# A transformer block on one core: rows and TensorE transposes in the first stage, loads a stage ahead and pinned uses at the end of attention

## The chip, the core and the metric

The kernel runs on one core of a Trainium2 chip. The core has engines that work side by side: TensorE (PE in the profile: matmuls and transposes, with its weight loads as PEld), VectorE (DVE), ScalarE (ACT), GpSimd (POOL), and SyncE (SP), whose queue issues most of the DMA transfers. [...] The metric is the device time of one execution in microseconds (us); the kernel before takes 1751.1 us, the median of three runs (1748.06 to 1751.12).

## The reference

One block on 2048 tokens of width 1024, in fp32: single-head attention of width 256 and a gated feed-forward network (FFN) of width 2752, each between two layer norms, with a residual.

```python
qkv = einsum('bsc,cf->bsf', x, Wqkv) + bqkv          # q, k, v of width 256
attn = softmax(einsum('bqd,bkd->bqk', q, k) / sqrt(d))
out  = einsum('bqk,bkd->bqd', attn, v) @ Wo + bo
# the block:
x = x + layernorm(attention(layernorm(x)))
x = x + layernorm((silu(xt @ W_gate.T) * (xt @ W_up.T)) @ W_down.T)   # xt = layernorm(x)
```

## The kernel before

**Precision.** A matmul operand is kept as two fp32r parts, a high part (an ACT cast, L109) and a low part (the difference, on DVE, L110); `split` makes both. A product is three matmuls: high x high, high x low, low x high (`mm3`, L142; `mmc`, L625).

**Order.** The program is traced in Python, and the framework then orders each engine's queue by simulating the traced program (`schedule_with_timeline_sim`, L1038): an instruction may be moved ahead of one traced earlier on its engine. `tc.keep_in_program_order(ins)` forbids this for one instruction: it stays behind the one traced just before it on its engine. Before the change only the last products of the second FFN product are kept so (L827). Buffers are given by hand: the same SBUF tiles (`f4`, `f2p`, `a1`, `a2`, `kx`, `wvo`, `qa`, `qb`, `xb`, `wr`, `xe`) serve one stage after another, and the eight PSUM banks are named at each use.

**Stage 1** (L240 to L254 and L337 to L354) normalizes x, transposes it to `xT` (channels on partitions, 512 tokens wide, double buffered by group), and computes K, Q (`qk`) and V (`v_block`) for four groups of 512 tokens (`g`). Group 0 comes by rows: `prep1` loads a tile of 128 tokens, normalizes its rows (`norm_rows`: bn_stats and aggregate on DVE, epsilon and the power on POOL, then L129), transposes it with eight PE transposes against the identity (L137) into two banks, and splits these. Groups 1 to 3 go another way, while PE works on the group before: `stats1` loads each of four tiles by rows for the statistics alone, and stores mean and reciprocal deviation to DRAM (`mr_d`, L198); `load_mr` reads the 512 pairs back, broadcast to all partitions (L202); `prep1t` then takes x already transposed by the host (`xt`), eight pieces of 128 channels x 512 tokens, subtracts the mean (L209, on POOL for odd pieces), multiplies (L210) and splits. The low parts of four Q and K weight blocks and of half the V weights are made by POOL.

**Attention** (L919 to L962) is a loop over 16 blocks `i` of 128 queries. Stage `i` transposes the probabilities of block `i` (`turn`, L292), computes scores and softmax of block `i + 1`, transposes the result of block `i - 1` (`turn_o`, L309), multiplies the probabilities by V (`attend`, L300, L301, and the sum of two halves at L304), and projects block `i - 1` (`proj`). For the first eight blocks (`EARLY`) the first residual and both norms follow at once (`residual`), and `xpose` transposes the normalized rows for the FFN and stores them to `xT_d`; the other eight leave their projection in `at_d`, and are finished beside the FFN's first pass.

**FFN** (L976 to L1001) runs in two passes over 1024 tokens each, with a Strassen-like scheme: `gate_up` makes seven block products for gate and for up from sums of x blocks (B11, B21, B22, T1 to T4), `run_down` the second product. Nearly all matmuls are at L628. The first pass's x blocks are made at the end of attention: `first_x` (stages 11 to 14) loads two pieces of `xT_d`, splits B11 and B21 into `xb`, forms sums (`sum_x`, L421) and stores them to `xs_d`; in stage 14 `first_t2` and `first_t13` reload sums and split them into `qa`, `qb`, `kx`; after the loop `first_t4` does so for T4 and B22 into `a1`, which holds V until attention is over. Four buffers (`spare`) serve these ten reloads in turn. Weights come through a feeder that loads and splits as buffers come free; two of its places lie in `wvo`, which `proj` uses to the end.

**Side work of the first pass.** Beside each of ten pairs of `gate_up`, `down_weights` loads two blocks of the down weights, forms four sums and stores them to `td`. In pairs 1 to 8 `late_tokens` finishes one of the eight late blocks: `residual` and, a step later, `xpose`. Loads and first uses stand in the same job.

Of the kernel before, what the change touches and what calls it, by code (L numbers as in the profile page):

```python
# [15 lines left out]
P = 128  # L16
# [17 lines left out]
@with_exitstack  # L34
def block_kernel(ctx, tc, x, xt, wqk, wv, bqk, bv, wo, bo, wgu, wlast, wd, out):

# [41 lines left out]
    dram = ctx.enter_context(tc.tile_pool(name="dram", bufs=1, space=bass.MemoryType.DRAM))  # L78
    mr_d = [tl(dram, [G, 2], F32, f"mr_d{g}") for g in range(NG)]
    q_d = [tl(dram, [P, 2, G], F32, f"q_d{g}") for g in range(NG)]  # L80
# [30 lines left out]

    def norm_stats(halves):

        s = small_tile()
        for i, h in enumerate(halves):
            nc.vector.bn_stats(s[:, 6 * i : 6 * i + 6], h)  # L116
        nc.vector.bn_aggr(s[:, 12:14], s[:, 0:12])
        nc.gpsimd.tensor_scalar(s[:, 14:15], s[:, 13:14], EPS, None, ALU.add)
        nc.gpsimd.tensor_tensor(s[:, 15:16], s[:, 14:15], mhalf, ALU.pow)
        return s[:, 12:13], s[:, 15:16], s  # L120
# [31 lines left out]
    vt = a1.rearrange("p a b c -> p (a b c)").rearrange("p (k h d) -> p k h d", h=2, d=D)  # L152
    xin, wraw, qst = f4[0:3], f4[3:5], f2[0:2]
    vst = [f2[4][:, 0:D], f2[4][:, D:]]
# [6 lines left out]
    def load_x(t):  # L161
        nc.sync.dma_start(xin[t % 3], x[t * P : (t + 1) * P, :])

# [3 lines left out]
    def load_wqk(i):  # L167
        r = wraw[raw_n[0] % 2].rearrange("p (c f) -> p c f", f=P)
        raw_n[0] += 1
        nc.scalar.dma_start(r, wqk[i])  # L170
        split(wqk_s[i][:, :, 0, :], wqk_s[i][:, :, 1, :], r, nc.gpsimd)

    def load_wv(i):
        r = wraw[raw_n[0] % 2].rearrange("p (c f) -> p c f", f=D)
        raw_n[0] += 1
        nc.scalar.dma_start(r, wv[:, 4 * i : 4 * i + 4, :])
        split(wv_s[:, 4 * i : 4 * i + 4, 0, :], wv_s[:, 4 * i : 4 * i + 4, 1, :], r, nc.gpsimd if i else nc.vector)

    def prep1(t, banks):
        norm_rows(xin[t % 3], t == 2)  # L180
        transpose_rows(xin[t % 3], xT[(t // TB) % 2], t % TB, banks)
        if t + 3 < TB:
            load_x(t + 3)

    xin_n = [0]
    xp = f2[2:4] + [f4[2][:, 0:512], f4[2][:, 512:1024]]
    xp_n = [0]

    def stats1(t):
        xt_ = xin[xin_n[0] % 2]
        xin_n[0] += 1
        nc.sync.dma_start(xt_, x[t * P : (t + 1) * P, :])
        m, r, s = norm_stats([xt_[:, 0:512], xt_[:, 512:1024]])
        nc.gpsimd.tensor_copy(s[:, 16:17], m)
        nc.gpsimd.tensor_copy(s[:, 17:18], r)
        nc.sync.dma_start(mr_d[t // TB][(t % TB) * P : (t % TB + 1) * P, :], s[:, 16:18])  # L198

    def load_mr(g):  # L200
        b = wraw[g % 2].rearrange("p (t s) -> p t s", s=2)
        nc.sync.dma_start(b, mr_d[g].partition_broadcast(P))  # L202
        return b

    def prep1t(g, c, mr):
        p = xp[xp_n[0] % 4]
        xp_n[0] += 1
        nc.sync.dma_start(p, xt[g, c])
        (nc.gpsimd if c % 2 else nc.vector).tensor_tensor(p, p, mr[:, :, 0], ALU.subtract)  # L209
        nc.vector.tensor_tensor(p, p, mr[:, :, 1], ALU.mult)  # L210
        d = xT[g % 2][:, c, :, :]
        split(d[:, 0, :], d[:, 1, :], p)

# [32 lines left out]
    load_wv(1)  # L246
    load_x(2)
    nc.scalar.dma_start(bv_s, bv.partition_broadcast(P))
    nc.scalar.dma_start(bqk_s, bqk)
# [37 lines left out]
    def turn(i, j):  # L287

        b = bank[4 + j % 2]
        for n in range(4):  # L290
            k = 4 * j + n
            nc.tensor.transpose(b[:, n * P : (n + 1) * P], p_s[:, k * P : (k + 1) * P], ident)  # L292
        d = pT[i % 2][:, 4 * j : 4 * j + 4, :, :]
        split(d[:, :, 0, :], d[:, :, 1, :], b.rearrange("p (n q) -> p n q", n=4))
# [11 lines left out]
    def turn_o(i):  # L306
        b = bank[7][:, 0:D]
        for d in range(2):
# [14 lines left out]
    def residual(t, a, xt):  # L323

        if t >= EARLY:
            nc.sync.dma_start(a, at_d[t])
            nc.sync.dma_start(xt, x[t * P : (t + 1) * P, :])
        m, r, s = norm_stats([a[:, 0:512], a[:, 512:1024]])
        nc.gpsimd.tensor_scalar(s[:, 16:17], m, r, -1.0, ALU.mult, ALU.mult)
# [7 lines left out]
    for g in range(NG):  # L337
        for i in range(4):
            qk(g, i, bank[4 + i % 2])
            if g + 1 == NG:  # L340
                continue
            if i == 0:
                for tb in range(TB):
                    stats1((g + 1) * TB + tb)
                mr = load_mr(g + 1)
            else:
                for c in range(2 * i - 2, 2 * i):
                    prep1t(g + 1, c, mr)
        if 0 < g < NG - 1:
            for tb in range(TB):  # L350
                v_block(g, tb, bank[6 + tb % 2])
        if g + 1 < NG:
            for c in range(6, 8):
                prep1t(g + 1, c, mr)  # L354
    x0_pool.release()
# [82 lines left out]

    def first_x(cb, r1, r2):
        load_xq(r1, 0, cb)  # L440
        load_xq(r2, 1, cb)
        split_xq(xb, cb, r1)
        sum_x(r1, r2)
        nc.sync.dma_start(xs_d[cb][0], r1)
        nc.sync.dma_start(xs_d[cb][1], r2)

    def first_t13(cb, r):
        nc.sync.dma_start(r, xs_d[cb][1])
        split_xq(kx, cb, r)

    def first_t2(n, r):
        for i in range(2):
            nc.sync.dma_start(r[:, (L, R)[i]], xs_d[2 * n + i][0][:, L])
        split(q2[n][:, :, 0, :], q2[n][:, :, 1, :], two(r))

    def first_t4(cb, r):
        nc.sync.dma_start(r[:, L], xs_d[cb][0][:, R])
        nc.sync.dma_start(r[:, R], xT_d[1][(4 + cb) * P : (5 + cb) * P, :])
        split_xq(a1, cb, r)

# [288 lines left out]

    bg_tiles = Ring(f4[0:4])  # L750

    def down_weights(p):

        r1, r2, r3 = (bg_tiles.get() for _ in range(3))
        nc.sync.dma_start(r1, wd[p * P : (p + 1) * P, :])
        nc.sync.dma_start(r2, wd[(p + NPAIR) * P : (p + NPAIR + 1) * P, :])
        add(r3[:, R], r2[:, R], r1[:, R], ALU.subtract)
        add(r3[:, L], r1[:, R], r1[:, L], ALU.subtract)
        add(r1[:, L], r3[:, R], r1[:, L])
        add(r2[:, L], r2[:, L], r1[:, L], ALU.subtract)  # L760
        for n, t in (("T1", r3[:, L]), ("T3", r3[:, R]), ("T2", r1[:, L]), ("T4", r2[:, L])):
            nc.sync.dma_start(td[p][n], t)
        for r in (r1, r2, r3):
            bg_tiles.free(r)

    def late_tokens(t, banks, part):
        if part == 0:
            late_tokens.tiles = bg_tiles.get(), bg_tiles.get()
            residual(t, *late_tokens.tiles)
        else:  # L770
            xpose(t, *late_tokens.tiles, banks)
            for r in late_tokens.tiles:
                bg_tiles.free(r)

# [144 lines left out]
    for i in range(NT):  # L919
# [10 lines left out]
        if more:  # L930
            scores(i + 1, 2)
            scores(i + 1, 3)
            softmax(i + 1)
        if 3 <= i < EARLY + 3:
            xpose(i - 3, *pair[(i - 3) % 3], bank[4:6])
        if i < EARLY:
            nc.sync.dma_start(pair[i % 3][1], x[i * P : (i + 1) * P, :])
        if i > 0:
            turn_o(i - 1)
        attend(i)  # L940
        if i > 0:
            proj(i - 1)
            if i - 1 < EARLY:
                residual(i - 1, *pair[(i - 1) % 3])
        if EARLY + 3 <= i < EARLY + 7:
            cb = i - EARLY - 3
            first_x(cb, *room[cb % 2])
# [26 lines left out]
    feed.pump()  # L974

    for s in range(2):  # L976
# [65 lines left out]
```

## Time and profile before

The profile is of one execution. Its parts used below: busy time of each engine, a row of 40 slices of the span, groups of instructions by line, and single instructions in order of time with what ended the idle time before them.

| | before |
|---|---|
| median of three runs | 1751.1 us |
| the profiled execution | 1749.74 us |
| its span, first to last instruction | 1748.0 us |
| mean granted TensorE clock | 0.986 |
| busy PE, PEld | 1698.3 us (97%), 1390.2 us (80%) |
| busy DVE, ACT, POOL | 1107.3, 694.5, 137.4 us |
| POOL busy in the first 120 us | 49 us |
| share of L628 in the chain that ended last | 69% |
| first attention transpose (L292) | 179.36 us |
| first FFN matmul (L628) | 441.7 us |
| last stall before L628 runs without a break | ends at 496.65 us |

The page's two rows on TensorE give the busy tenths of each of 40 equal slices (43.7 us each), and the granted clock in tenths:

```profile
PE   8789999998889999999999999999999999999997
PEclk9899999999999999999999999999999999999999
```

A matmul row's mean is the time from start to end of one matmul; neighbours overlap, so their spacing is shorter. The clock is what the throttle granted: at half of it matmuls follow each other at about half the rate.

### The profile page before, as it was taken

How to read it: one execution, taken by the hardware profiler on the slowest of the kernel's cores; microseconds unless marked ns; L12 is line 12 of the kernel's file. 1: busy time of each engine (PE TensorE's matmuls, PEld its weight loads, DVE VectorE, ACT ScalarE, POOL GpSimd, SP SyncE). 2: the span in 40 equal slices, each digit the busy share in tenths (PEclk: the TensorE clock that was granted, in tenths of full speed). 3: DMA queues.
4: the chain of work that ended last, by engine and by line, in shares of the span. 5: the costliest groups of instructions: out<-in, count | busy, mean ns of one | idle time of the engine just before them, and what ended most of it. 6: DMA issues, size and time to landing. Idle time of an engine off the chain costs nothing.

```text
span 1748.0 us, 21019 instructions
## 1 busy us (share of the span) xinstructions
PE 1698.3 (97%) x7692; PEld 1390.2 (80%) x7692; DVE 1107.3 (63%) x1636; ACT 694.5 (40%) x1032; POOL 137.4 (8%) x208
## 2 busy tenths in 40 slices
PE   8789999998889999999999999999999999999997
PEld 6578888887778888888888888788888888888886
DVE  6682577757667777777458546875655565355458
ACT  3131455535434444443245444333333333244343
POOL 5320001100011111111000001100000000000001
PEclk9899999999999999999999999999999999999999
DMA  7741023346365556665447656732333223386664
GB/s 224 176 134 49 13 76 99 123 156 224 115 231 179 187 187 234 205 218 189 160 137 255 212 178 198 246 100 97 105 128 112 96 91 115 121 280 197 193 188 160
DMA packets 136056, 278.89 MB, mean 160 GB/s; under 512 B 15376, under 2 KB 31888, under 8 KB 135952
## 3 DMA queue, kind: packets, MB, share of 16 engines
q1 hardware_dynamic: 133216, 270.60, 47.7%
q10 hardware_dynamic: 2736, 6.95, 1.1%
q8 instruction: 60, 0.98, 0.2%
q14 instruction: 44, 0.36, 0.1%
HBM read 193.60 MB, written 83.90 MB: 159 GB/s over the span
## 4 chain that ended last, share of the span: by engine, by line
PE 86%; DMA 7%; DVE 5%; issue 1%; ACT 1%; POOL 0%; DVEq 0%; POOLq 0%; SPq 0%; ACTq 0%
PE bank L628 69%; PE bank L144 3%; PE bank L145 3%; PE bank L146 3%; PE bank L300 3%; PE bank L301 1%; PE bank L231 1%; PE bank L292 1%; DMA mr_d<-small 1%; PE bank L384 1%; DVE small L116 1%; DVE a L110 1%; DMA f<-xT_d 1%; PE bank L232 1%; DMA f<-wd 1%
## 5 line engine op out<-in xcount | busy, mean ns | idle before, releaser
L628 PE MATMUL bank<-a 128*128 128x512 f32 x1176 | 273.7, 390 | 0.0
L628 PEld LDWEIGHTS bank<-a 128*128 128x128 f32 x1176 | 220.7, 188 | 46.9
L110 DVE TENSOR_TENSOR a<-f2p,a 128x1024 fp32r<-128x1024 f32 (+2 forms) x122 | 137.3, 1126 | 101.3 <-ACT a L109 89.3
L628 PE MATMUL bank<-xb,a 128*128 128x512 f32 x816 | 197.3, 395 | 0.0
L641 DVE TENSOR_TENSOR xi<-bank,xi 128x512 f32<-128x512 f32 (+1 forms) x168 | 113.3, 685 | 114.5 <-PE bank L628 52.5
L628 PEld LDWEIGHTS bank<-xb,a 128*128 128x128 f32 x816 | 152.9, 188 | 37.1
L109 ACT CAST a<-f2p 128x1024 fp32r<-128x1024 f32 (+2 forms) x122 | 112.9, 928 | 160.6 <-PE bank L628 108.5
L628 PE MATMUL bank<-kx,a 128*128 128x512 f32 x648 | 158.2, 395 | 0.0
L628 PE MATMUL bank<-a,a 128*128 128x512 f32 x648 | 155.6, 392 | 0.0
L628 PEld LDWEIGHTS bank<-kx,a 128*128 128x128 f32 x648 | 121.5, 187 | 29.4
L628 PE MATMUL bank<-wvo 128*128 128x512 f32 x600 | 142.4, 390 | 0.0
L628 PEld LDWEIGHTS bank<-a,a 128*128 128x128 f32 x648 | 121.1, 188 | 26.0
L628 PEld LDWEIGHTS bank<-wvo 128*128 128x128 f32 x600 | 112.6, 188 | 24.4
L110 DVE TENSOR_TENSOR a<-f,a 128x512 fp32r<-128x512 f32 (+3 forms) x103 | 86.8, 847 | 69.3 <-ACT a L109 65.8
L109 ACT CAST a<-f 128x512 fp32r<-128x512 f32 (+3 forms) x103 | 76.2, 742 | 135.6 <-PE bank L628 100.9
L628 PE MATMUL bank<-a,wvo 128*128 128x512 f32 x384 | 96.3, 400 | 4.6 <-DVE xi L641 4.6
L300 PE MATMUL bank<-a,a 128*128 128x512 f32 x256 | 97.3, 412 | 2.6 <-ACT a L109 2.6
L110 DVE TENSOR_TENSOR wvo<-f2p,wvo 128x1024 fp32r<-128x1024 f32 (+2 forms) x47 | 53.4, 1137 | 63.2 <-ACT wvo L109 54.6
L110 DVE TENSOR_TENSOR a<-wr,a 128x1024 fp32r<-128x1024 f32 (+2 forms) x62 | 65.2, 1053 | 43.1 <-ACT a L109 26.1
L628 PE MATMUL bank<-kx,wvo 128*128 128x512 f32 x384 | 91.6, 390 | 0.0
L628 PEld LDWEIGHTS bank<-a,wvo 128*128 128x128 f32 x384 | 73.1, 191 | 22.4 <-DVE xi L641 5.0
L641 DVE TENSOR_TENSOR xi<-xi,xi 128x512 f32<-128x512 f32 x124 | 85.2, 687 | 3.6
(236 smaller groups left out, 2796.3 us busy)
## 6 DMA issues: line engine op xcount, KB each, us to landing
f2p<-wgu SPq DMA_DIRECT2D x43, 512.0 KB, 4.3
hd_S<-xi SPq DMA_DIRECT2D x80, 256.0 KB, 5.2
f<-x SPq DMA_DIRECT2D x30, 512.0 KB, 5.7
hd_A<-xi SPq DMA_DIRECT2D x60, 256.0 KB, 2.0
f<-wgu SPq DMA_DIRECT2D x21, 512.0 KB, 5.2
wr<-wgu SPq DMA_DIRECT2D x20, 512.0 KB, 5.3
f<-wd SPq DMA_DIRECT2D x20, 512.0 KB, 4.8
td_T<-f SPq DMA_DIRECT2D x40, 256.0 KB, 3.1
```

The lines of the kernel that those rows point to most:

```text
L109: nc.scalar.copy(hi, src)
L110: (lo_engine or nc.vector).tensor_tensor(lo, src, f32(hi), ALU.subtract)
L116: nc.vector.bn_stats(s[:, 6 * i : 6 * i + 6], h)
L144: nc.tensor.matmul(o, w[0], m[0], start=first, stop=False)
L145: nc.tensor.matmul(o, w[0], m[1], start=False, stop=False)
L146: nc.tensor.matmul(o, w[1], m[0], start=False, stop=last)
L231: nc.tensor.matmul(b, xg[:, c, 0, cols], wv_s[:, c, :, :].rearrange("p a f -> p (a f)"), start=(c == 0), stop=False)
L232: nc.tensor.matmul(b[:, D:], xg[:, c, 1, cols], wv_s[:, c, 0, :], start=False, stop=(c == 7))
L292: nc.tensor.transpose(b[:, n * P : (n + 1) * P], p_s[:, k * P : (k + 1) * P], ident)
L300: nc.tensor.matmul(b, p[:, k, 0, :], vt[:, k, :, :].rearrange("p h d -> p (h d)"), start=(k == 0), stop=False)
L628: one = nc.tensor.matmul(o, w[i], m[j], start=first and n == 0, stop=last and n == 2, skip_group_check=chained)
L641: nc.vector.tensor_tensor(o, a, b, op)
```

## The change

Stage 1 takes every group by rows. `stats1`, `load_mr`, `prep1t`, `mr_d` and the host's `xt` go; `prep1` serves all 16 tiles, four buffers of x are loaded at the start, and tile `t + 4` is loaded as soon as tile `t` has been transposed. The tiles of group `g + 1` are prepared one after each `qk(g, i)`. The epsilon is added on DVE, and all low parts of weights are made on DVE.

In attention the banks are dealt out anew: `turn` uses 4 and 7, `turn_o` 5, and `xpose`, now for block `i - 2` and after the projection, 6 and 5. The reloads for the first pass become objects with a `load` and a `use`; the uses are pinned. `first_x` is cut into `first_load`, a stage ahead, and `first_sums`. Four reloads are issued in stage 14 and used in stage 15 ahead of `attend(15)`; two are loaded and used right behind the loop, the last four behind `proj(15)`.

Beside the first pass, `load_down(p + 1)` and `residual` run in the second job of pair p (`behind`), while `xpose` of the block before, the loads for the next late block and the sums of `down_weights` run in its first job (`ahead`); `down_weights` works in place in two buffers, with its first subtraction pinned, and `residual` of late blocks has its bn_stats pinned.

```diff
-    def norm_stats(halves):
+    def norm_stats(halves, pin=None):
...
-            nc.vector.bn_stats(s[:, 6 * i : 6 * i + 6], h)
+            b = nc.vector.bn_stats(s[:, 6 * i : 6 * i + 6], h)
+            if pin:
+                pin(b)
...
-        nc.gpsimd.tensor_scalar(s[:, 14:15], s[:, 13:14], EPS, None, ALU.add)
+        nc.vector.tensor_scalar(s[:, 14:15], s[:, 13:14], EPS, None, ALU.add)
...
-    xin, wraw, qst = f4[0:3], f4[3:5], f2[0:2]
+    xin, wraw, qst = f4[0:4], [f4[4], f2p[1]], f2[0:2]
...
-        split(wqk_s[i][:, :, 0, :], wqk_s[i][:, :, 1, :], r, nc.gpsimd)
+        split(wqk_s[i][:, :, 0, :], wqk_s[i][:, :, 1, :], r)
...
     def prep1(t, banks):
-        norm_rows(xin[t % 3], t == 2)
-        transpose_rows(xin[t % 3], xT[(t // TB) % 2], t % TB, banks)
-        if t + 3 < TB:
-            load_x(t + 3)
...
+        r = xin[t % TB]
+        norm_rows(r, False)
+        transpose_rows(r, xT[(t // TB) % 2], t % TB, banks)
+        if t + TB < NT:
+            load_x(t + TB)
...
             qk(g, i, bank[4 + i % 2])
...
+            if g + 1 < NG:
+                prep1((g + 1) * TB + i, (bank[2 * (i % 2)], bank[2 * (i % 2) + 1]))
...
-        b = bank[4 + j % 2]
+        b = bank[(4, 7)[j % 2]]
...
-        b = bank[7][:, 0:D]
+        b = bank[5][:, 0:D]
...
+    def split_later(dst, src):
+        pin(nc.scalar.copy(dst[:, :, 0, :], src))
+        pin(nc.vector.tensor_tensor(dst[:, :, 1, :], src, f32(dst[:, :, 0, :]), ALU.subtract))
...
+    class First:
+        def __init__(self, dst, halves):
+            self.dst, self.halves = dst, halves
+        def load(self, r):
+            self.r = r
+            for h, d in zip((L, R), self.halves):
+                nc.sync.dma_start(r[:, h], d)
+        def use(self):
+            split_later(self.dst, two(self.r))
...
     def down_weights(p):
-        r1, r2, r3 = (bg_tiles.get() for _ in range(3))
-        nc.sync.dma_start(r1, wd[p * P : (p + 1) * P, :])
-        nc.sync.dma_start(r2, wd[(p + NPAIR) * P : (p + NPAIR + 1) * P, :])
-        add(r3[:, R], r2[:, R], r1[:, R], ALU.subtract)
...
+        r1, r2 = f4[0:2]
+        pin(nc.vector.tensor_tensor(r2[:, R], r2[:, R], r1[:, R], ALU.subtract))
...
-        if 3 <= i < EARLY + 3:
-            xpose(i - 3, *pair[(i - 3) % 3], bank[4:6])
...
             turn_o(i - 1)
+        if i == NT - 1:
+            for f in order[:4]:
+                f.use()
         attend(i)
         if i > 0:
             proj(i - 1)
...
+        if 2 <= i < EARLY + 2:
+            xpose(i - 2, *pair[(i - 2) % 3], (bank[6], bank[5]))
+        if 0 < i <= EARLY:
+            residual(i - 1, *pair[(i - 1) % 3])
+        cb = i - EARLY - 3
+        if 0 <= cb < 4:
+            first_sums(cb, *room[cb % 2])
+        if 0 <= cb + 1 < 4:
+            first_load(cb + 1, *room[(cb + 1) % 2])
...
+            order = [t2[0], t13[0], t13[1], t13[2], t2[1], t13[3]] + t4
             spare = f4[2], f4[3], wr[1], xe
-            for n in range(2):
-                first_t2(n, spare[n])
-            for cb in range(4):
-                first_t13(cb, spare[(2 + cb) % 4])
-    for cb in range(4):
-        first_t4(cb, spare[(2 + cb) % 4])
+            for f, r in zip(order, spare):
+                f.load(r)
+    for n in range(4, 6):
+        order[n].load(spare[n % 4])
+        order[n].use()
     turn_o(NT - 1)
     proj(NT - 1)
+    for n in range(6, 10):
+        order[n].load(spare[n % 4])
+        order[n].use()
...
+    def ahead(p):
+        if late(p - 1):
+            xpose(late(p - 1), *f4[2:4], Y[0:2])
+        if late(p):
+            nc.sync.dma_start(f4[2], at_d[late(p)])
+            nc.sync.dma_start(f4[3], x[late(p) * P : (late(p) + 1) * P, :])
+        down_weights(p)
+    def behind(p):
+        if p + 1 < NPAIR:
+            load_down(p + 1)
+        if late(p):
+            residual(late(p), *f4[2:4])
+    load_down(0)
...
-            jobs = []
-            if s == 0:
-                jobs.append(lambda: down_weights(p))
-                if 1 <= p < 1 + NT - EARLY:
-                    t = EARLY + p - 1
-                    jobs += [lambda: late_tokens(t, Y[0:2], 0), lambda: late_tokens(t, Y[0:2], 1)]
+            jobs = [] if s else [lambda: ahead(p), lambda: behind(p)]
```

More of the change, by code (lines that the diff above doesn't have):

```diff
@@ L34, in block_kernel @@
 @with_exitstack
-def block_kernel(ctx, tc, x, xt, wqk, wv, bqk, bv, wo, bo, wgu, wlast, wd, out):
+def block_kernel(ctx, tc, x, wqk, wv, bqk, bv, wo, bo, wgu, wlast, wd, out):
     nc = tc.nc
@@ L78, in block_kernel @@
     dram = ctx.enter_context(tc.tile_pool(name="dram", bufs=1, space=bass.MemoryType.DRAM))
-    mr_d = [tl(dram, [G, 2], F32, f"mr_d{g}") for g in range(NG)]
     q_d = [tl(dram, [P, 2, G], F32, f"q_d{g}") for g in range(NG)]
@@ L161, in load_x @@
     def load_x(t):
-        nc.sync.dma_start(xin[t % 3], x[t * P : (t + 1) * P, :])
+        nc.sync.dma_start(xin[t % TB], x[t * P : (t + 1) * P, :])
     raw_n = [0]
@@ L176, in load_wv @@
         nc.scalar.dma_start(r, wv[:, 4 * i : 4 * i + 4, :])
-        split(wv_s[:, 4 * i : 4 * i + 4, 0, :], wv_s[:, 4 * i : 4 * i + 4, 1, :], r, nc.gpsimd if i else nc.vector)
+        split(wv_s[:, 4 * i : 4 * i + 4, 0, :], wv_s[:, 4 * i : 4 * i + 4, 1, :], r)
     def prep1(t, banks):
-        norm_rows(xin[t % 3], t == 2)
-        transpose_rows(xin[t % 3], xT[(t // TB) % 2], t % TB, banks)
-        if t + 3 < TB:
-            load_x(t + 3)
[L187 to L212, printed above, removed]
+        r = xin[t % TB]
[3 more added lines that the diff above has]
+            load_x(t + TB)
     def qk(g, i, b):
@@ L247, in block_kernel @@
     load_x(2)
+    load_x(3)
     nc.scalar.dma_start(bv_s, bv.partition_broadcast(P))
@@ L323, in residual @@
     def residual(t, a, xt):
[L325 to L328, printed above, removed]
+        m, r, s = norm_stats([a[:, 0:512], a[:, 512:1024]], tc.keep_in_program_order if t >= EARLY else None)
         nc.gpsimd.tensor_scalar(s[:, 16:17], m, r, -1.0, ALU.mult, ALU.mult)
@@ L339, in block_kernel @@
             qk(g, i, bank[4 + i % 2])
[L340 to L348, printed above, removed]
+            if g + 1 < NG:
+                prep1((g + 1) * TB + i, (bank[2 * (i % 2)], bank[2 * (i % 2) + 1]))
         if 0 < g < NG - 1:
@@ L351, in block_kernel @@
                 v_block(g, tb, bank[6 + tb % 2])
-        if g + 1 < NG:
-            for c in range(6, 8):
-                prep1t(g + 1, c, mr)
     x0_pool.release()
@@ L436, in build_x, with first_load, first_sums @@
         split_x("T4", cb, r1[:, R])
-    def first_x(cb, r1, r2):
+    pin = tc.keep_in_program_order
+    def split_later(dst, src):
+        pin(nc.scalar.copy(dst[:, :, 0, :], src))
+        pin(nc.vector.tensor_tensor(dst[:, :, 1, :], src, f32(dst[:, :, 0, :]), ALU.subtract))
+    def first_load(cb, r1, r2):
         load_xq(r1, 0, cb)
         load_xq(r2, 1, cb)
-        split_xq(xb, cb, r1)
+    def first_sums(cb, r1, r2):
+        split_later(by_half(xb)[:, :, cb], two(r1))
         sum_x(r1, r2)
@@ L445, in first_x @@
         nc.sync.dma_start(xs_d[cb][1], r2)
[L447 to L459, printed above, removed]
+    class First:
[7 more added lines that the diff above has]
+            split_later(self.dst, two(self.r))
+    t13 = [First(by_half(kx)[:, :, cb], (xs_d[cb][1][:, L], xs_d[cb][1][:, R])) for cb in range(4)]
+    t2 = [First(q2[n], (xs_d[2 * n][0][:, L], xs_d[2 * n + 1][0][:, L])) for n in range(2)]
+    t4 = [First(by_half(a1)[:, :, cb], (xs_d[cb][0][:, R], xT_d[1][(4 + cb) * P : (5 + cb) * P, :])) for cb in range(4)]
     class Ring:
@@ L748, in gate_up_rest, with load_down @@
         nc.sync.dma_start(hl_d[s][1], g22[:FR, :])
-    bg_tiles = Ring(f4[0:4])
+    def load_down(p):
+        for r, fb in zip(f4[0:2], (p, p + NPAIR)):
+            nc.sync.dma_start(r, wd[fb * P : (fb + 1) * P, :])
     def down_weights(p):
-        r1, r2, r3 = (bg_tiles.get() for _ in range(3))
-        nc.sync.dma_start(r1, wd[p * P : (p + 1) * P, :])
-        nc.sync.dma_start(r2, wd[(p + NPAIR) * P : (p + NPAIR + 1) * P, :])
-        add(r3[:, R], r2[:, R], r1[:, R], ALU.subtract)
-        add(r3[:, L], r1[:, R], r1[:, L], ALU.subtract)
-        add(r1[:, L], r3[:, R], r1[:, L])
+        r1, r2 = f4[0:2]
+        pin(nc.vector.tensor_tensor(r2[:, R], r2[:, R], r1[:, R], ALU.subtract))
+        add(r1[:, R], r1[:, R], r1[:, L], ALU.subtract)
+        add(r1[:, L], r2[:, R], r1[:, L])
         add(r2[:, L], r2[:, L], r1[:, L], ALU.subtract)
-        for n, t in (("T1", r3[:, L]), ("T3", r3[:, R]), ("T2", r1[:, L]), ("T4", r2[:, L])):
+        for n, t in (("T1", r1[:, R]), ("T3", r2[:, R]), ("T2", r1[:, L]), ("T4", r2[:, L])):
             nc.sync.dma_start(td[p][n], t)
[L763 to L773, printed above, removed]
     def wd_half(fb, j):
@@ L942, in block_kernel @@
             proj(i - 1)
[L943 to L947, printed above, removed]
+        if 2 <= i < EARLY + 2:
[7 more added lines that the diff above has]
+            first_load(cb + 1, *room[(cb + 1) % 2])
         if i == NT - 4:
@@ L974, in block_kernel, with late @@
     feed.pump()
+    def late(p):
+        return EARLY + p if 0 <= p < NT - EARLY else None
+    def ahead(p):
[11 more added lines that the diff above has]
+    load_down(0)
     for s in range(2):
@@ L1022 @@
         "x": x.reshape(T, C),
-        "xt": x.reshape(NG, G, NC_, P).transpose(0, 2, 3, 1),
         "wqk": blocks(np.concatenate([w[:, D : 2 * D], w[:, :D]], axis=1)),
```

## The prediction

> **What bounds the kernel now.** I read the page's 40 slices first, for where TensorE (PE) is not full; then a table of windows over those stretches; then the waits of PE; then single rows of the timeline for what stands in front of a late instruction. In the slices PE reads 9 nearly everywhere, so only work that PE itself does, or time in which it does none, can change the end.
>
> The windows: length in us, then busy us (instructions) of PE, weight load, VectorE (DVE), ScalarE (ACT), GpSimd (POOL), then the granted clock, DMA share, GB/s.
>
> ```profile
> 40.00:60.00 20.00, 15.01 (x56) 11.05 (x54) 10.34 (x19) 1.68 (x3) 6.99 (x18) 0.91 0.79 156
> 60.00:80.00 20.00, 14.34 (x51) 10.52 (x52) 18.48 (x30) 5.98 (x10) 10.80 (x19) 0.82 0.63 161
> 80.00:100.00 20.00, 15.08 (x50) 11.72 (x50) 14.73 (x24) 4.41 (x9) 6.38 (x7) 0.76 0.60 157
> 180.00:380.00 200.00, 199.59 (x1105) 169.02 (x1103) 132.11 (x257) 101.33 (x208) 16.96 (x48) 1.00 0.27 85
> 380.00:400.00 20.00, 18.03 (x86) 14.82 (x85) 16.00 (x30) 7.08 (x16) 0.00 (x0) 0.91 0.73 263
> ...
> 420.00:440.00 20.00, 15.05 (x71) 12.12 (x71) 12.15 (x20) 9.74 (x19) 0.00 (x0) 0.83 0.48 158
> ...
> 460.00:480.00 20.00, 14.98 (x61) 11.25 (x60) 14.83 (x21) 10.24 (x15) 0.00 (x0) 0.91 0.66 218
> 480.00:500.00 20.00, 15.42 (x62) 12.20 (x61) 13.49 (x21) 7.06 (x10) 1.68 (x3) 0.91 0.57 192
> ```
>
> A window's loss is its idle PE time plus (1 - clock) x length: in the half-clock stretches the L300/L301 pairs follow each other at 0.64 us, elsewhere at 0.35. From 40 to 100 us: 6.8 + 9.3 + 9.7 = 25.8. From 380 to 500 us: 3.8 + 0 + 8.4 + 0 + 6.8 + 6.4 = 25.4. Counting matmuls at their warm spacing (0.233 us for 512 columns) gives 26 and 23. Attention proper, 180 to 380, loses 0.4, and 520 to 1700 nothing: the change can gain only in two places, and everything it adds to PE elsewhere is paid in full.
>
> What PE waited for (total us, times, longest):
>
> ```profile
> PE bank L144 <- DVE kx L221: 5.5, 3, 3.4
> PE bank L628 <- DVE xi L641: 4.6, 1, 4.6
> PE bank L309 <- DVE f L304: 4.4, 2, 2.7
> PE bank L144 <- ACT kx L220: 3.6, 1, 3.6
> ...
> PE bank L231 <- ACT a L109: 3.0, 1, 3.0
> PE bank L300 <- ACT a L109: 2.6, 1, 2.6
> ```
>
> The L144 and L231 waits lie in 40 to 100 us, the others in 380 to 500. None of the engines named is saturated there; each stood behind a transfer. In group order: the four `mr_d` stores and the broadcast reload land in 6.6 and 5.1 us after each x load's 5.7, so each group's statistics cost 17 us of DMA in series before `prep1t` may start.
>
> **Stage 1, removed.** Per group of 512 tokens DVE did 8 bn_stats and 4 aggregates (5.9 us), some 4 subtractions at L209 (1.13 us mean), 8 multiplications at L210 (0.78), 8 low parts (0.62): 21.7 us. The L209 and L210 means are stretched by POOL's share of L209, as the first row shows:
>
> ```profile
> 57.30 1.83 DVE L209 TENSOR_TENSOR f2p<-f2p,f 128x512 f32<-128x512 f32 x1 [2.73 <-DMA f<-mr_d]
> ...
> 24.84 1.09 PE L137 MATMUL bank<-ident,f 128*128 128x128 f32 x8
> 25.68 0.37 PE L232 MATMUL bank<-wvo,xT 128*128 128x256 f32 x1
> ```
>
> **Stage 1, put in.** Per 128 tokens: bn_stats 1.28, aggregate 0.20, an epsilon add now on DVE (some 0.1, the nearest row being L281's 0.15), L129 0.81, two low parts 1.3: 3.7 us, 14.7 a group. The pow stays on POOL, and ACT makes the same eight casts a group. x is loaded a whole group ahead (PE needs 22 to 37 us a group, a load 5.7), so the DMA chain is gone, and SP issues 39 transfers less (12 `mr_d`, 3 reloads, 24 `xt`). `load_x(t+4)` holds SP until tile t is transposed; behind it stand only q_d stores and later x loads. The first 2 us still ask for 2 MB of x (four loads for three and two `xt`). The five low parts of weights that POOL did come to DVE: 5 x 1.21 = 6 us, all before 40 us.
>
> PE gets 12 x 8 = 96 transposes. The rows above price them: eight occupy PE from 24.84 to 25.68, where the next matmul starts, 0.105 us each, so 10.1 us. [...] This trace also has a mean of 272 to 292 ns in its transpose rows, but as latency, overlapped by the neighbours. [...] And attention has 281 transposes (L292 195, L384 64, L309 22) between 180 and 380 with the clock at 1.00: mixed with matmuls they do not lower it. I take 10.1.
>
> What is late next: the border from group 0 to group 1. DVE starts at 6.3 us and owes 4 x 3.7 for group 0, 7.3 for weights, 5.0 for four V epilogues, 14.7 for group 1, 2.7 for Q and K epilogues: 44.5, so 50.8 without a pause, some 54 with 3 us of waiting for data. PE, at 48.3 when it ran dry before, has 3.4 us of transposes more: 51.7. I take 3 us of loss, with half-clock time 4 (ends 0 and 8). From there a group costs PE 37.0 us (24 x 4 x 0.233 + 11.2 + 3.4) and DVE 21 (14.7 + 5.0 + 1.3), so PE has the cover; 1 us (0 to 4). The first 20 us, 9.5 lost until the first x is normalized, stay.
>
> Stage 1: 25.8 - 4 - 1 - 10.1 = **10.7 us gained**. Ends: 25.8 - 0 - 10.1 = +16, and 25.8 - 12 - 10.1 = +4[...].
>
> **End of attention.** The waits one by one, by what stood ahead in the engine's queue:
> - 387.5, 1.97 us: DVE's L304 stood behind L421 waiting for `load_xq` (landed at 387.55). Loads go a stage (16.8 us of PE) ahead, against 4 to 6 us of landing: gone, with 1.8 us of half clock.
> - 423.3, 1.76 us: L304 stood behind low parts for T1, T3 and T2, 1.22 us each. Four of the six move to stage 15, behind `turn_o(14)`, two behind the loop: gone here.
> - 429.2, 2.6 + 0.6 us, and 3.4 of clock: ACT's pT cast stood behind a cast whose reload had not landed:
>
> ```profile
> 430.19 1.04 ACT L109 CAST kx<-f 128x1024 fp32r<-128x1024 f32 x1 [2.94 <-DMA f<-xs_d]
> 431.14 0.58 ACT L109 CAST a<-bank 128x512 fp32r<-128x512 f32 x1
> ```
>
>   Issued in stage 14, used in stage 15: gone.
> - 462.6, 2.7 + 0.5 us, and 1.8 of clock: L304 stood behind four T4 splits. They are pinned behind `proj(15)`: gone.
> - 470.5, 1.9 us: `g11`'s copy (L660) behind two casts of weights into `wvo`. Untouched; stays.
> - 492.1, 4.6 us, and 1.8 of clock: DVE in `gate_up`'s first pair stood behind `down_weights` and `residual`, whose loads were issued at their use (2.4 + 5.0 + 2.3 us of DVE waiting). With loads a half-pair or more ahead (PE needs 39 us a pair): gone.
>
> New waits: `order[4]` and `[5]` are loaded into `spare[0:2]` and used at once. ACT's cast waits for the landing, with `turn_o(15)`'s cast possibly behind it, and then `proj(15)`, the `wvo` slots and their weights. The load can start once use 0 is through DVE (1.05 + 1.22 us) and takes 4.3 us (longest 5.8), 8 in all; PE's cover is attend(15) and proj(14), 16 x 0.35 + 2.8 = 8.4, plus up to 48 products on B11 and B21 (11 us). Cost with cover 0; without it 5.8 and a 3.4 us half-clock window, 7.5. Six of the ten splits also crowd ACT and DVE just before FFN weights do. T4 is needed 28 us into the FFN, so 6 to 9 are covered. I take 4 (nearer the covered case, as the cover is ample), which with L660's 1.9 leaves about 6. The gain, from the smaller count: 23 - 6 = **17 us**; ends 7 and 22. On SP's queue `load_down(0)` must wait for the `at_d` stores from f4[0:2], but is used only a quarter pair later.
>
> The rest: `down_weights` keeps its four additions, `xpose` its transposes, `turn` and `turn_o` swap banks: 0, hidden by DVE's and ACT's idle third and half of attention.
>
> **Sum.** 10.7 + 17 = 27.7. The profiled execution took 1749.7 us (span 1748.0 and 1.7 around it): 1722. The median of the runs is 1.4 above it: **1723**.
>
> **Rivals.**
> - *Only stage 1 gains*: the pinned uses hold ACT and DVE in order before late data, and the end's stalls move behind the loop. For: two uses directly follow their loads. Against: the covers above. 10.7 + 3: **1737**.
> - *Only the end gains*: DVE becomes stage 1's bound (44.5 of 45 us at its start)[...]. Against: 14.7 us a group, less than the 21.7 of before. 17 + 0: **1734**.
> - *Slower: banks.* `turn` now shares bank 7 with `proj`, and `xpose` shares 6 with `attend` and 5 with `turn_o` and `proj`. If an evacuation (ACT 0.59 + DVE 0.68 = 1.3 us) is exposed at two of these handovers in 14 stages, 36 us come in where only 0.4 was lost: **1759**. It decides from 2.0 us a stage. Against: bank 5 had turns, proj and xpose before, with PE full at 16.8 us a stage.
> - *Everything goes*, nothing new waits: 16 + 22: **1713**.
>
> **How the numbers follow.** Forecast 0.58, with its own range 1714 to 1732; only stage 1 0.14; only the end 0.13; everything 0.05; banks 0.07; the gains just cancelled 0.03. Dropping the banks' 0.07, the cancelled 0.03 and the outer halves of others leaves 1712 to 1739. Two runs of this kernel can be told apart from some 0.2% (3.5 us) on: faster 0.90; the cancelled case splits into within 0.02 and slower 0.01, so slower is 0.08.
>
> **What would show it.** Right: 40 to 100 us with PE near 20 of 20 and clock 1.00, no `mr_d`, POOL nearly idle there, the first L292 some 10 us earlier; 0.1 us per L137; the start of solid L628 some 27 us earlier; none of the six waits but L660's. Wrong: DVE solid and PE waiting for xT's low parts up to 60 us; PE idle beside `turn_o` after the loop; any loss inside attention.

## The result, and the profile after

The changed kernel takes 1727.2 us (median of four runs, 1727.15 to 1728.61), the kernel before 1749.6 beside it. The ratio is 0.9875, 95% interval 0.9858 to 0.9892: 22 us or 1.25% faster. The forecast was 1723.

First the windows of the profile after (span 1726.8 us; columns as in the prediction):

```profile
20.00:40.00 20.00, 19.01 (x100) 15.41 (x100) 19.87 (x41) 8.91 (x15) 3.48 (x5) 1.00 0.55 185
40.00:60.00 20.00, 20.00 (x111) 16.97 (x110) 14.35 (x28) 6.24 (x12) 2.44 (x4) 1.00 0.21 69
60.00:80.00 20.00, 20.00 (x97) 16.41 (x96) 11.02 (x23) 2.90 (x6) 1.80 (x3) 1.00 0.19 64
...
180.00:360.00 180.00, 176.78 (x971) 148.25 (x971) 117.33 (x246) 88.81 (x185) 13.01 (x32) 1.00 0.29 94
...
440.00:460.00 20.00, 13.69 (x40) 9.65 (x40) 17.12 (x22) 12.41 (x17) 0.00 (x0) 0.66 0.67 231
460.00:480.00 20.00, 20.00 (x89) 16.29 (x88) 17.08 (x28) 9.33 (x14) 2.30 (x3) 1.00 0.65 232
```

Stage 1 is clean: PE is busy 20.00 us of every 20, at a granted clock of 1.00, from 40 to 160 us, and POOL is nearly idle. Of the losses before the FFN one hole is left, at 440 to 460: by the rule of the prediction 6.3 us idle and (1 - 0.66) x 20 = 6.8 us lost to the clock, 13.1 in all. And attention, which lost 0.4 us in 200, now idles 3.2 in 180.

The waits of PE in the same trace name both (total us, times, longest), and PE's rows in the hole show four pauses:

```profile
PE bank L604 <- ACT xi L636: 3.4, 1, 3.4
PE bank L138 <- DVE f L130: 3.3, 2, 3.0
PE bank L145 <- DVE oTs L109: 2.2, 2, 1.8
PE bank L275 <- ACT f L348: 2.0, 2, 1.4
```

```profile
442.44 0.44 PE L284 MATMUL bank<-ident,f 128*128 128x128 f32 x2 [0.26 <-DVE f L279]
443.82 0.50 PE L145 MATMUL bank<-wvo,oTs 128*128 128x512 f32 x1 [0.94 <-ACT oTs L108]
...
446.31 0.80 PE L145 MATMUL bank<-wvo,oTs 128*128 128x512 f32 x1 [1.76 <-DVE oTs L109]
...
454.29 2.93 PE L604 MATMUL bank<-qa,a 128*128 128x512 f32 x6 [3.35 <-ACT xi L636]
```

L604 is the FFN's matmul line now (L628 before), L636 is `g11`'s copy (L660), L145 to L147 are `mm3`, L284 is `turn_o`, L275 is `attend`, L348 the copy in `xpose`, L406 and L407 the high and low part of a pinned use, L428 the load of a `First`, L728 that of `load_down`.

Three marks read from PE's timeline divide the gain: the start of the last V matmul, the start of the last matmul of `attend`, the end of the last matmul.

| us | before | after | difference |
|---|---|---|---|
| stage 1: to the last V matmul | 186.5 | 172.3 | -14.2 |
| attention: from there to the last `attend` | 274.5 | 268.2 | -6.2 |
| the rest: from there to the last matmul | 1277.7 | 1277.0 | -0.7 |

Stage 1 gave 14.2 us against 10.7 predicted; all that lies behind it gave 7.0 against 17. The last row is the surprise, and the rule of the windows accounts for it. Behind the last `attend` PE lost 9.6 us idle and 3.4 to the clock before, and loses 6.3 and 6.8 now: 13.0 and 13.1. The stall of 4.6 us in `gate_up`'s first pair is gone. But PE waits for `turn_o(15)` and its splits 3.0 us, where it had waited 3.1, and for `g11`'s copy 3.4, where it had waited 1.9; and the clock costs twice as much.

The chain that ended last, in the profile after, from the end of attention (start us, us, what):

```profile
443.07 2.75 DMA at_d<-f
...
445.88 0.33 SPq L728
...
446.31 0.38 SPq L428
...
446.74 5.89 DMA f<-xT_d
...
452.71 1.04 ACT a L406
453.75 0.49 ACT xi L636
454.25 0.04 issue
454.29 2.93 PE bank L604 x6
```

Read backwards: PE waits for `g11`'s copy, which stands on ACT behind a pinned cast (use 9), which waits for its reload, which was issued on SP behind the first down-weight load, which waits until `at_d` has been stored from the same buffer. Two of these links are queue order alone: the copy doesn't need the cast, yet starts at 453.75 us, where the cast's 1.04 us from 452.71 end; nor does the reload need the down-weight load. The second of them is short. The last reader of the reload's buffer, DVE's low part of use 5, ended at 445.91 us, so the reload could have gone out 0.4 us earlier at most.

### The profile page after: what moved, and what is told of

It is laid out like the page before. It is cut to its first block, busy times and chain, and to the rows that moved or that the text cites. A ratio compares the mean times of both kernels' runs of the same rounds, so it can differ in the third digit from the quotient of the medians.

```text
span 1726.8 us, 21119 instructions
## 1 busy us (share of the span) xinstructions
PE 1699.3 (98%) x7788; PEld 1393.6 (81%) x7788; DVE 1091.8 (63%) x1666; ACT 689.1 (40%) x1031; POOL 89.0 (5%) x118
## 4 chain that ended last, share of the span: by engine, by line
PE 93%; DVE 3%; DMA 2%; issue 1%; ACT 1%; POOL 0%; SPq 0%; POOLq 0%; DVEq 0%; ACTq 0%
PE bank L604 70%; PE bank L146 4%; PE bank L145 4%; PE bank L147 4%; PE bank L275 3%; PE bank L276 2%; PE bank L267 1%; PE bank L205 1%; PE bank L206 1%; PE bank L346 1%; DMA f<-x 1%; PE bank L138 1%; DVE small L115 0%; PE bank L773 0%; PE bank L774 0%
## 5 line engine op out<-in xcount | busy, mean ns | idle before, releaser
L604 PE MATMUL bank<-a 128*128 128x512 f32 x1176 | 273.8, 390 | 0.0
L604 PEld LDWEIGHTS bank<-a 128*128 128x128 f32 x1176 | 220.8, 188 | 46.8
L604 PE MATMUL bank<-xb,a 128*128 128x512 f32 x816 | 197.3, 395 | 0.0
L109 DVE TENSOR_TENSOR a<-f2p,a 128x1024 fp32r<-128x1024 f32 (+2 forms) x114 | 124.7, 1095 | 93.4 <-ACT a L108 81.0
L604 PEld LDWEIGHTS bank<-xb,a 128*128 128x128 f32 x816 | 152.9, 187 | 37.1
L604 PE MATMUL bank<-kx,a 128*128 128x512 f32 x648 | 157.1, 395 | 0.0
L604 PE MATMUL bank<-a,a 128*128 128x512 f32 x648 | 153.4, 390 | 0.0
L108 ACT CAST a<-f2p 128x1024 fp32r<-128x1024 f32 (+2 forms) x114 | 107.6, 949 | 112.5 <-PE bank L604 102.4
L109 DVE TENSOR_TENSOR a<-f,a 128x512 fp32r<-128x512 f32 (+3 forms) x93 | 91.3, 981 | 91.4 <-ACT a L108 88.0
L604 PEld LDWEIGHTS bank<-kx,a 128*128 128x128 f32 x648 | 121.5, 187 | 29.5
L604 PEld LDWEIGHTS bank<-a,a 128*128 128x128 f32 x648 | 121.6, 188 | 26.4
L604 PE MATMUL bank<-wvo 128*128 128x512 f32 x600 | 142.4, 390 | 0.0
L604 PEld LDWEIGHTS bank<-wvo 128*128 128x128 f32 x600 | 112.6, 188 | 24.4
L108 ACT CAST a<-f 128x512 fp32r<-128x512 f32 (+3 forms) x93 | 69.4, 747 | 125.7 <-PE bank L604 90.6
L275 PE MATMUL bank<-a,a 128*128 128x512 f32 x256 | 94.5, 402 | 2.8 <-ACT f L348 2.0
L604 PE MATMUL bank<-a,wvo 128*128 128x512 f32 x384 | 93.7, 396 | 1.2 <-ACT xi L663 1.2
L604 PE MATMUL bank<-kx,wvo 128*128 128x512 f32 x384 | 91.9, 390 | 0.0
L604 PEld LDWEIGHTS bank<-a,wvo 128*128 128x128 f32 x384 | 72.0, 188 | 18.8 <-ACT xi L663 1.6
L604 PEld LDWEIGHTS bank<-kx,wvo 128*128 128x128 f32 x384 | 72.1, 188 | 15.7
```

The costliest lines, as they stand in the source:

```text
L108: nc.scalar.copy(hi, src)
L109: (lo_engine or nc.vector).tensor_tensor(lo, src, f32(hi), ALU.subtract)
L275: nc.tensor.matmul(b, p[:, k, 0, :], vt[:, k, :, :].rearrange("p h d -> p (h d)"), start=(k == 0), stop=False)
L604: one = nc.tensor.matmul(o, w[i], m[j], start=first and n == 0, stop=last and n == 2, skip_group_check=chained)
```

## The experiments

Theory: the two halves of the change each give what the marks say, stage 1 because PE no longer waits for DMA round trips, and the end less than predicted because pinned uses hold ACT and DVE in front of the critical instructions behind the loop. Rival: the loads a stage ahead are what helps and the pins are idle, or the stall behind the loop is the chain of attention itself, which no order shortens. Times of one group are medians beside the kernel before on the same chip.

**Each half alone.** `e1_stage1` takes only the parts of the diff up to `prep1` and the loop that calls it; `e2_end` all the others, with the epsilon left on POOL.

> Stage 1 alone is changed (rows, TensorE transposes, epsilon and low parts on VectorE); attention, its end and the side work stay as before. The ledger of the two traces puts 14.2 us of the gain into this stage (the last V matmul ends 14.2 us earlier). Theory, the stages add up: 1735 to 1737 us, with the stall of 440 to 500 us of the kernel before kept, about 14 us earlier. Rival, the time won early is partly lost again at the end of attention because the same loads and stalls wait there: less than 8 us gained, 1742 or more.

> All but stage 1 is changed: banks of attention, reloads with pinned uses, side work of the first pass; stage 1 as before. The ledger leaves 7.0 us for this part. Theory: 1742 to 1744 us. The prediction's step had 17 us for it, 1733. Rival, the two parts need each other (the end gains only when stage 1 is early): no gain at all, 1749 or more.

Measured: stage 1 alone 1731.1 us (before 1749.0; ratio 0.9895, 0.9881 to 0.9910), 17.9 gained; the end alone 1738.9 (0.9938, 0.9921 to 0.9955), 10.1 gained. Both gain on their own, and by more than the marks gave them. Together they make 28.0, and the change as a whole, 0.9875 of 1749.0, only 21.9: 6 us are lost in company (9 by the 0.9889 of `e12_again` below; the intervals leave either figure uncertain by some 5). By the marks, stage 1 alone is 13.3 us shorter up to the last V matmul, 1.8 in attention, where the waits for `turn_o` are still there (5.8 us idle in the last 70 us), and 3.3 in the rest. The end alone is 8.1 us shorter in attention and 1.6 in the rest. So the last row of the table is no property of the uses: the end alone has them too, and gains 1.6 there. Nor is the clock's share constant: from 440 to 460 us it was 0.66 in the changed kernel, with 6.3 us of idle PE, and 0.76 in `e12_again` below, with 7.1.

**What a transpose costs.** 96 more of them, into the same place:

```diff
-                nc.tensor.transpose(b[:, j * P : (j + 1) * P], t[:, cb * P : (cb + 1) * P], ident)
+                for _ in range(times):     # 2 for t >= TB
+                    nc.tensor.transpose(b[:, j * P : (j + 1) * P], t[:, cb * P : (cb + 1) * P], ident)
```

> The changed kernel with each of the 96 transposes of groups 1 to 3 issued twice into the same place. If a transpose costs its spacing of 0.105 us among matmuls, 10 us are added, 1737 us; if it costs its latency of about 0.275 us, 26 us, 1753 us; if the engine had slack in the stage, under 4 us. The granted clock from 40 to 160 us should stay at 1.00[...].

Measured: 1737.7 us, 0.9933 (0.9918 to 0.9947) of before, so 10.6 above the changed kernel's 0.9875; the last V matmul starts 10.8 us later, 0.113 us for each transpose. Windows between 40 and 160 us of this run, its row of the transposes in 40 to 165, and a stretch of them:

```profile
40.00:60.00 20.00, 20.00 (x110) 16.91 (x109) 12.16 (x26) 4.56 (x9) 2.41 (x4) 1.00 0.17 53
60.00:80.00 20.00, 20.00 (x114) 17.11 (x113) 11.52 (x20) 5.50 (x9) 1.75 (x3) 1.00 0.25 73
...
140.00:160.00 20.00, 20.00 (x95) 16.50 (x94) 5.19 (x9) 3.14 (x5) 0.00 (x0) 1.00 0.17 54
```

```profile
L139 PE MATMUL bank<-ident,f 128*128 128x128 f32 x176 | 20.8, 273 | 0.0
```

```profile
59.71 3.66 PE L139 MATMUL bank<-ident,f 128*128 128x128 f32 x32
63.12 0.48 PE L206 MATMUL bank<-wvo,a 128*128 128x512 f32 x1
```

The mean is 273 ns and the price 113: the mean counts the time that a transpose spends overlapped with its neighbours. The clock stays at 1.00 in all six windows, through 3.4 us of nothing but transposes too (59.71 to 63.12).

**The pins.** `e3_nopin` makes every new pin an ordinary instruction; `e3u_nopin_uses` only those in `split_later`, which are the ten uses and also the four splits of `first_sums`.

```diff
-        m, r, s = norm_stats([a[:, 0:512], a[:, 512:1024]], tc.keep_in_program_order if t >= EARLY else None)
+        m, r, s = norm_stats([a[:, 0:512], a[:, 512:1024]], None)
...
-    pin = tc.keep_in_program_order
+    pin = lambda ins: ins
```

> The changed kernel with every new pin taken away, so that the framework may order the uses, the first subtraction of the down weights and the late bn_stats as it likes; the loads are still issued ahead. If the pins hold the gain: waits behind loads come back in 370 to 500 us, 1734 us or more. If the loads ahead do it and the pins only move the stall behind the loop (turn_o's cast and g11's copy behind uses that are held in order): 1722 to 1728 us, the same or faster.

> The changed kernel with only the pins of the ten uses taken away; those of the side work (first subtraction of the down weights, late bn_stats) stay. The run without any pin lost 2 us up to the last attend and 14 us after it. Theory, the side work's pins are what holds the gain, since there a load is still in flight when the framework thinks it landed, while the uses' pins trade one stall for another: 1727 to 1731 us. Rival, the uses' pins hold it: 1736 or more.

Without any pin: 1741.9 us (0.9959, 0.9944 to 0.9974), two thirds of the gain lost. In the profiled execution (1744.6 us) the part behind the last `attend` is 14.1 us longer. The waits behind loads did come back, but later than the expected 370 to 500 us: DVE's waits from 500 to 700 us show what a pin on its queue had kept away. With the pins it waits there for no transfer at all:

```profile
DVE f L733 <- DMA f<-wd: 7.1, 3, 4.0
DVE small L115 <- DMA f<-at_d: 6.5, 4, 2.4
```

With only `split_later` unpinned: 1727.4 us (1725.5 to 1728.3) where the changed kernel, run beside it (`e12_again`), took 1730.0 (1727.9 to 1731.0), 1 us above its expected range.

> The changed kernel as it is, once more, beside the others on their chip, as their measure: 1727 to 1729 us. Nothing is told apart by it alone.

So the pins of the side work carry 14 us, and those of `split_later` nothing: beside `e12_again` attention gets 2.6 us longer without them and the rest 6.4 shorter. They trade one stall for another. The rival of `e3_nopin` (the loads ahead do it, and pins only move a stall) was right about the uses and wrong about the side work, whose first DVE instructions, when they aren't pinned, stand waiting for loads still in flight.

**Taking the uses out of the way.** `e4_turn_first` lets `turn_o(15)` go first, `e5_t4_later` moves two T4 uses into the first side job:

```diff
     for n in range(4, 6):
         order[n].load(spare[n % 4])
-        order[n].use()
     turn_o(NT - 1)
+    for n in range(4, 6):
+        order[n].use()
     proj(NT - 1)
```

```diff
-    for n in range(6, 10):
+    for n in range(6, 8):
         order[n].load(spare[n % 4])
         order[n].use()
+    for n in range(8, 10):
+        order[n].load(spare[n % 4])
...
     def ahead(p):
+        if p == 0:
+            order[8].use()
+            order[9].use()
```

> The changed kernel with the two uses that directly follow their loads (T2's second half and the last T1/T3) moved behind turn_o(15). In the changed kernel the wait of proj(15) for oTs (0.9 + 1.8 us) stands behind these two splits on ScalarE and VectorE. Theory, the pinned uses hold up the end: the oTs waits go, 2.7 us, and with them part of the 13.7 us at half clock: 1719 to 1724 us. Rival, they only move on to g11's copy (L636), the next thing on ScalarE: 1726 to 1728.

> The changed kernel with the last two T4 uses moved into the first side job of the first pair, behind g11's copy in trace order. In the changed kernel g11's copy (L636) waits 3.35 us behind two casts of weights and a pinned cast whose load landed at 452.7 us. Theory: the last cast no longer stands in front, the wait falls to some 2 us as in the kernel before, and the half-clock time by one window or two: 1722 to 1726 us. Rival, the two casts of weights bind anyway: 1727.

Both missed: 1727.6 us (0.9888, 0.9867 to 0.9908) and 1728.4 (0.9896, 0.9879 to 0.9914), no change. In `e4` the wait for oTs is gone as expected (0.46 us is left of 2.70), and the wait of L604 has grown from 3.35 to 9.55. ACT in that run:

```profile
448.08 1.05 ACT L108 CAST wvo<-f 128x1024 fp32r<-128x1024 f32 x1
455.19 1.04 ACT L406 CAST a<-f 128x1024 fp32r<-128x1024 f32 x1 [6.05 <-DMA f<-xT_d]
456.14 0.58 ACT L636 COPY xi<-bank 128x512 f32<-128x512 f32 x1
```

The later use frees its buffer later (at 446.3 us, where it was 444.2), and the next reload of that buffer goes out later still: at 449.1, where it was 444.2. In between it stood on SP behind the first down-weight load, which waited for `at_d`'s store until 448.6. And the use of that reload stands before `g11`'s copy. In `e5` both moved casts were still ordered in front of the copy (they start at 449.0 and 454.0, the copy at 454.9; 4.8 us of wait): moving a call down in the program isn't moving it in the queue.

`e11_down_behind` took `e4` and put `load_down(0)`, pinned, behind the reloads on SP.

> The run with the two uses behind turn_o(15), and besides load_down(0) pinned on SyncE's queue behind the last reloads. In that run g11's copy came to wait 9.6 us: the reloads of the last T4 blocks stood on SyncE behind the first down-weight load, which waits until at_d has been stored from the same buffer. Theory, this queue is the cause: the reloads go out some 3 us earlier, the copy's wait falls to 4 us or less, 1719 to 1723 us. Rival, the loads wait for the buffers that the late uses hold: no change, 1727.

1728.3 us, no change, but not for the rival's reason alone. Counted from the last `attend`, the reloads were issued 2.8 us earlier than in `e4`, as the theory had it: at 447.4 and 448.5, as soon as DVE had ended the low parts that read the buffers. The copy still waited 8.6 us, since the framework now ordered both T4 casts in front of it (one in `e4`), and the second one's reload took from 448.9 to 455.2. With the uses late, SP's order cost 2.8 us and the buffers are the limit behind it; in the changed kernel itself SP's order costs 0.4 at most (the chain above).

**A version that does it.** `e9_slots` has both moves, and gives the two weight buffers in `wvo` free only in the first side job; `e10_best` also has `load_down(0)` behind the reloads and one T4 use more in that job.

```diff
-    for n in range(2):
-        slots.free(flat(wvo[:, 2 * n : 2 * n + 2, :, :]))
     feed.pump()
...
     def ahead(p):
+        if p == 0:
+            order[8].use()
+            order[9].use()
+            for n in range(2):
+                slots.free(flat(wvo[:, 2 * n : 2 * n + 2, :, :]))
+            feed.pump()
```

> Both of these moves, and the two weight buffers in wvo are given free only in the first side job, so that the third pair of weight splits takes the buffers of the first products and g11's copy has no weight cast for proj(15)'s buffer ahead of it. Theory, the whole stall behind the loop (6.3 us idle, 6.8 us by the clock) is made of queue order: at most 3 us of it is left, 1713 to 1720 us. Rival, the chain attend, turn_o, proj, split is what the stall is, and the order moves it about: 1723 or more.

> The run with both moves and the wvo buffers freed later, and besides load_down(0) pinned behind the reloads and one more T4 use moved into the first side job. Theory, each cast taken out of ScalarE's row before g11's copy shortens the 3.5 us wait by its 1.0 us, and a shorter stop leaves out the half-clock window: 1718 to 1722 us. Rival, the copy then waits for a weight cast whose load has not landed, since its load went behind the reloads: 1723 or more.

`e9` took 1723.1 us (0.9867, 0.9850 to 0.9885), `e10` 1723.1 (0.9852, 0.9836 to 0.9868), the latter beside the changed kernel's 1730.0 (0.9889, 0.9873 to 0.9906), the runs of the two without overlap. Both miss their expected range, by 3 and 1 us, and stand on the border of their rivals (1723 or more). `e9` lies 4.5 us below `e4`, which ran beside it, without overlap either. The rest behind `attend` is 5 us shorter than in the changed kernel. The window of `e10`, the same columns:

```profile
440.00:460.00 20.00, 16.69 (x64) 12.04 (x63) 16.93 (x23) 14.74 (x21) 0.00 (x0) 0.91 0.70 246
```

Here 3.3 us are idle and 1.8 lost to the clock; with 1.6 us idle in the next window (a wait for ACT's copy at L659) that makes 6.7 of 13.1. The theory holds in its direction: about half of the hole was queue order. It fell short of the 3 us: `g11`'s copy (at 448.5 us in `e10`) follows eight casts that run without a break from 442.9 on, so ACT is full there. Three of the eight are uses; whether they could go behind the copy as well wasn't tried. Nor were the two moves without the `wvo` buffers, so which part of `e9` does it is open; what `e10` adds shows no gain over `e9`.

**Banks.** `e8_xbank` deals `xpose` the banks 7 and 5.

```diff
-            xpose(i - 2, *pair[(i - 2) % 3], (bank[6], bank[5]))
+            xpose(i - 2, *pair[(i - 2) % 3], (bank[7], bank[5]))
```

> The changed kernel with xpose in banks 7 and 5 instead of 6 and 5, so that attend no longer waits for the evacuation of xpose's bank. In the changed kernel TensorE stood 2.0 us in two such waits (L275 behind L348) between 180 and 380 us, where it lost 3.2 us in all against 0.4 before. Theory, the bank dealt to xpose is the cost: 2 us gained, 1725. Rival, bank 7 is needed by the next turn and the wait moves there: 1727 or more.

1734.1 us (0.9929, 0.9915 to 0.9944), 7 us worse. PE's waits in this run from 180 to 380 us:

```profile
PE bank L275 <- ACT a L108: 5.0, 7, 0.7
PE bank L145 <- ACT p_s L258: 1.1, 6, 0.2
```

The wait for L348 is gone, and PE waits seven times, up to 0.7 us, for pT's cast of a `turn`, whose bank 7 now also waits for `xpose`. The rival again, and a small measure of the prediction's rival on banks: a handover moved from bank 6 to bank 7 makes attention 6.3 us longer.

## Why the prediction was right, and where not

- **Stage 1, 10.7 predicted, 14.2 measured.** Mechanism and sign as forecast. The 96 transposes, put at 10.1, cost 10.6 to 10.8. The term that was mis-sized is "the border from group 0 to group 1", with what follows it 5 us: DVE was as full as reckoned (19.87 of 20 us between 20 and 40), but PE lost 1.0 us there and nothing after, since the framework had interleaved V's matmuls of group 0 with Q and K's, so that PE had work while DVE caught up. The 26.7 us lost from 20 to 100 fell to 1.0; the first 20 us lost 1.1 more.
- **End of attention, 17 predicted, 7.0 measured.** The three stalls before the last `attend` went, as the steps said: no idle PE in the last 70 us before it, where 5.0 had been. `down_weights`' stall at 492 went too, and the pins there are worth 14 us, more than the step knew. Two steps failed. The first is the one on 462.6, "They are pinned behind `proj(15)`: gone". The T4 splits left, but uses 4 and 5 took their place in front of `turn_o(15)`'s cast and low part, and PE waits 3.0 us there instead of 3.1; `e4`, with these two moved behind `turn_o(15)`, has 0.7. The second is "I take 4 (nearer the covered case, as the cover is ample), which with L660's 1.9 leaves about 6": the hole behind the loop is 13.1 us. Its idle part, 6.3, is near the estimate. The clock is what was mis-sized: it cost 6.8 us where one stretch of 3.4 us at 0.50, 1.7 us of loss, was allowed for at most. And the cover was not there: the 48 products on B11 and B21, counted as cover, had been placed by the framework before the last `attend` ended (L604 runs between 421 and 437 us in the chain), as they had been in the trace of before (from 441.7). In the prediction's own sum, 23 less 13.1 and less the 2.8 us more that PE idles inside attention is 7.1.
- **"0, hidden by DVE's and ACT's idle third and half of attention"** for the banks: 3.2 us idle where 0.4 was, 2.0 of them at L275 behind `xpose`'s copy from bank 6. The rival on banks was real, at a tenth of its price. The end alone has 0.4 us of this wait, with the same banks, so the banks alone don't set it.
- **Transposes, priced by their spacing.** Each took 0.113 us in the queue of `e6`, against a mean of 273 ns in its row (292 in L137's row of before). At 273 ns the 96 would have cost 26.2 us, more than the 25.8 that the stage had lost. The clock stayed at 1.00 through the 3.4 us of transposes alone in `e6`.
- **The rivals.** "Only stage 1 gains" came nearest in its mechanism: the stall did move behind the loop. Its size (3 us left for the end) was too low. The total lay within the range because a stage estimated 3.5 us too low and one 10 too high partly cancelled.

What stays open: the 6 us that the two halves lose in company. By the marks, the two alone save 9.9 us in attention and 4.9 behind it, and together 6.2 and 0.7. Which order of the queues makes the difference wasn't isolated; the last section shows how unequal the clock's share was beside like sums of idle time.

## What to carry to other kernels

Price an instruction on a full engine by the start of its neighbour, never by its row's mean: here that is 0.11 against 0.27 us, and it decides the sign of the edit. Where a framework orders queues greedily, work counted as cover for a later stall is spent earlier: look in the trace where it lies before counting on it. A pin helps where a load is in flight (14 us here); a pinned use right in front of the critical instruction only changes what that instruction waits for. Moving two such uses gained nothing here (`e4`, `e5`); the run that moved all four and the release of two weight buffers gained 4.5 us over `e4`.

## What the runs showed of the hardware

In the changed kernel the granted clock was 1.00 from 20 to 445.5 us, 0.50 from there to 459.15 (13.7 us), and 1.00 again up to 1700. At 0.50 the matmuls of L145 to L147 on 512 columns started 0.43 us apart (446.90, 447.33, 447.75), at 1.00 0.23 (440.62, 440.85, 441.09). In the 3.4 us before 445.5 PE had been idle for 0.26 us, for 0.94, and for the first 0.94 of the pause of 1.76: 2.1 us in all, with work in between. The pause of 3.4 lies inside the half-clock stretch, and so 6.3 us of idle time cost 13.1.

In the kernel before, the clock was 0.50 four times between 380 and 500 us:

| clock 0.50, us | length, us | pause of PE ahead of it or across its start, us |
|---|---|---|
| 390.4 to 393.8 | 3.4 | 1.97, up to 389.5 |
| 431.3 to 438.2 | 6.8 | 2.61, up to 431.8 |
| 465.5 to 468.9 | 3.4 | 2.68, up to 465.3 |
| 496.2 to 499.6 | 3.4 | 4.58, up to 496.65 |

Two more pauses between 380 and 500 us, of 1.76 us up to 425.0 and of 1.87 up to 472.4, had 1.00 behind them, for 6.3 and 23.8 us. So the longest pause alone doesn't tell the clock in these two traces: 1.87 us in one piece came with none of the half clock, and 0.26, 0.94 and 1.76 close together with 13.7 us of it. Nor does the sum of the pauses: behind attention 9.6 us of idle PE came with 3.4 lost to the clock in the kernel before, and 6.3 with 6.8 in the changed one. In `e12_again` the window from 440 to 460 us has 7.1 us idle and, at its 0.76, 4.8 lost. What sets the length of a half-clock stretch wasn't isolated.
